# Attention scores: the low-part products of two heads on half the rows each, and both heads' score tiles filled together

## The chip, the cores and the metric

The kernel runs on 1 core of a Trainium2 chip. The metric is the device time of one execution, in microseconds. A core has a matrix engine (TensorE, PE in the profile; PEld is its weight load), VectorE (DVE), ScalarE (ACT), GpSimd (POOL), and a queue that issues DMAs (SyncE, SP). Each engine works through its own queue of instructions in order, and they wait for each other by semaphores.

## The reference, cut to what matters

The input `x` is 4 sequences of 1024 tokens of 256 numbers. Four residual blocks follow each other: a linear recurrence, a sparse feed-forward block (FFN), attention with 8 heads of 64, and the same FFN again. The change lies in the attention:

```python
q = (x @ Wq.T).reshape(b, t, N_HEADS, HEAD_DIM)
kv_latent = x @ Wkv_down.T                              # 64 numbers for each token
k = (kv_latent @ Wk_up.T).reshape(b, t, N_HEADS, HEAD_DIM)
v = (kv_latent @ Wv_up.T).reshape(b, t, N_HEADS, HEAD_DIM)
scores = jnp.einsum('bqhd,bkhd->bhqk', q, k) * HEAD_DIM ** (-0.5)
attn = jax.nn.softmax(scores, axis=-1)
out = jnp.einsum('bhqk,bkhd->bqhd', attn, v)
return out.reshape(b, t, N_HEADS * HEAD_DIM) @ Wo.T
```

## The kernel before

The kernel folds `Wk_up` into the query weights, so that all heads share one set of keys: the 64 latents of each token. For accuracy every factor of a product is split into a high part that TensorE multiplies exactly (`kh`) and the rest, a low part (`kl`). The latents are produced twice, one copy above the other, so `kh` and `kl` are tiles of 128 partitions by 1024 tokens whose halves hold the same 64 latents. The queries of one head `j` of a pair are a tile `qs[:, j, :]`, whose 64 rows of this head (rows 0 to 63 for `j = 0`, 64 to 127 for `j = 1`) hold the high part and whose other 64 rows hold the low part. A product `qs.T @ kh` over 128 rows is therefore (high + low of the queries) times the high part of the keys, and `qs.T @ kl` the same queries times the low part of the keys.

`Attention.heads` runs over the tokens of one sequence: 2 blocks of 512 tokens, 4 pairs of heads `g`, 4 query tiles `q` of 128 tokens; in all 128 such steps for the 4 sequences, each with two heads `j`, and so 256 score tiles. For one head the steps are:

- L881: four matmuls fill a score tile `sc` of 128 queries by 1024 keys in PSUM (two banks): two column halves `kb` with `kh`, then the two halves with `kl`. There are two buffers of `sc`.
- L885: VectorE takes the negated row maximum `nm`. For even `q`, L887 adds a constant to it.
- L889: ScalarE writes `pr`, the exponentials, and their sums. After this the `sc` buffer is free.
- Even `q` (`by_dma`): L892 and L893 split `pr` into two f16 parts `pd` on ScalarE and GpSimd, and L894 transposes them by DMA into `d`. Odd `q`: L900 transposes `pr` on TensorE into `ptp`, and L903 or L905 copies it into `p`.
- `values_sum` (L925) multiplies by the latents into `pmo` for both heads, the two heads in the two column halves of TensorE; L933 transposes the reciprocals of the sums into the same bank, L935 copies them, and L936 scales the result into `on`. It runs one step late.

Between these steps a generator schedule (`merge`) lets side work in: the FFN tiles `f1.tile` (top-32 search on VectorE, L674; products L170, L556), preparation of the next sequence, queries (`pmq`, L170; `qs`, L853), the output product (`pmy`, L170). The order in which the program is written is not yet the order of the queues: a scheduler that plays the program through a timeline decides the order of each engine's queue. `tc.high_priority()` raises the priority of what is issued in it, and `tc.issue_after(x)` puts an instruction behind `x` in the queue's order.

Of the kernel before, what the change touches and what calls it, by code (L numbers as in the profile page):

```python
# [21 lines left out]
P = 128  # L22
B = 4
T = 1024
# [6 lines left out]
HD = 64  # L31
# [148 lines left out]
class Banks:  # L180


    def __init__(self, pool, bufs):
        self.pool, self.bufs = pool, bufs
# [587 lines left out]

class Attention:
    def __init__(self, tc, x, ident, ident64, wqk, wvo, wd, sp, wp):
        self.nc, self.x, self.ident, self.ident64 = tc.nc, x, ident, ident64
        self.wqk, self.wvo, self.wd, self.sp, self.wp = wqk, wvo, wd, sp, wp
        self.hp = None
        self.k, self.xnt, self.qs, self.on = {}, {}, {}, {}

        self.sident = wp.tile([HD, HD], F32R, tag="sident", name="sident")  # L780
# [75 lines left out]
    def heads(self, b, psum):  # L856

        nc, sp, wp = self.nc, self.sp, self.hp  # L860
        kh, kl, la, lb = self.k[b]
        late, pending = [], []
        for nb, g, q in ((nb, g, q) for nb in range(2) for g in range(PAIRS) for q in range(4)):
            by_dma = q % 2 == 0
            if g == 0:
                self.on[b, nb, q] = wp.tile([P, PAIRS, P], F32, tag=f"on{q}", name=f"on{q}")
            qs = self.qs[b, nb, g]
            ssum = sp.tile([P, 2], F32, tag="ssum", name="ssum", bufs=4)
            if by_dma:
                pts = [wp.tile([P, 2 * TPB, P], F16, tag=f"d{j}", name=f"d{j}", bufs=2) for j in range(2)]  # L870
                parts = ((0, lb[0]), (TPB, lb[0]), (0, lb[1]))
                terms = [(v[:, c, :], i + c) for c in range(TPB) for i, v in parts]
            else:
                pts = [wp.tile([P, TPB, P], F32, tag=f"p{j}", name=f"p{j}") for j in range(2)]
                terms = [(la[:, c, :], c) for c in range(TPB)]
            for j in range(2):
                sc = psum.tile([P, T], "sc", "sc")
                for i, kk in enumerate((kh, kl)):
                    for kb in range(2):
                        sl = slice(kb * 512, (kb + 1) * 512)  # L880
                        nc.tensor.matmul(  # L881
                            sc[:, sl], qs[:, j, q * P : (q + 1) * P], kk[:, sl], start=(i == 0), stop=(i == 1)
                        )
                nm = sp.tile([P, 1], F32, tag="nm", name="nm", bufs=4)
                nc.vector.tensor_reduce(nm, sc, AX.X, ALU.max, negate=True)  # L885
                if by_dma:
                    nc.vector.tensor_scalar(nm, nm, PSHIFT * math.log(2.0), None, ALU.add)  # L887
                pr = wp.tile([P, T], F32, tag="pr", name="pr", bufs=3)
                nc.scalar.activation(pr, sc, AF.Exp, bias=nm, accum_out=ssum[:, j : j + 1])  # L889
                if by_dma:  # L890
                    pd = wp.tile([P, 2, T], F16, tag="pd", name="pd", bufs=2)
                    nc.scalar.copy(pd[:, 0, :], pr)  # L892
                    nc.gpsimd.tensor_tensor(pd[:, 1, :], pr, pd[:, 0, :], ALU.subtract)  # L893
                    nc.sync.dma_start_transpose(pts[j], pd.rearrange("p i k -> p (i k)"))  # L894
                else:
                    for half in range(2):
                        pt = psum.tile([P, 4, P], "t", "ptp")
                        for kk in range(4):
                            kc = 4 * half + kk
                            nc.tensor.transpose(pt[:, kk, :], pr[:, kc * P : (kc + 1) * P], self.ident)  # L900
                        dst = pts[j][:, 4 * half : 4 * half + 4, :]
                        if half == 0 and b == B - 1:
                            nc.vector.tensor_copy(dst, pt)  # L903
                        else:
                            nc.scalar.copy(dst, pt)  # L905
                if j == 0 and pending:
                    self.values_sum(*pending.pop(0), psum)
                if j == 1 and late and by_dma:
                    self.values_sum(*late.pop(0), psum)
                yield  # L910
            (late if by_dma else pending).append((pts, terms, ssum, self.on[b, nb, q][:, g, :]))
        for args in late + pending:
            self.values_sum(*args, psum)

    def values_sum(self, pts, terms, ssum, on, psum):

        nc, sp = self.nc, self.sp
        rs = sp.tile([P, 2], F32, tag="rs", name="rs")
        nc.vector.reciprocal(rs, ssum)
        rows = sp.tile([P, 2, HD], F32, tag="rows", name="rows")  # L920
        nc.gpsimd.tensor_copy(rows, rs[:, :, None].to_broadcast([P, 2, HD]))  # L921
        po = psum.tile([P, 2, P], "s", "pmo")
        for n, (v, c) in enumerate(terms):
            for j in range(2):
                nc.tensor.matmul(  # L925
                    po[j * HD : (j + 1) * HD, 0, :],
                    v,
                    pts[j][:, c, :],
                    start=(n == 0),
                    stop=(n == len(terms) - 1),  # L930
                )

        nc.tensor.transpose(po[:, 1, :], rows.rearrange("p j d -> p (j d)"), self.ident)  # L933
        rb = sp.tile([P, P], F32, tag="rb", name="rb", bufs=1)
        nc.scalar.copy(rb, po[:, 1, :])  # L935
        nc.vector.tensor_tensor(on, po[:, 0, :], rb, ALU.mult)  # L936
# [370 lines left out]
```

## Time and profile before

| | |
|---|---|
| median of 3 runs | 1532.92 us (1526.67 to 1534.85) |
| the profiled execution's own time | 1534.08 us |
| its span, first to last instruction | 1532.4 us |
| granted TensorE clock, mean | 0.937 of full speed |
| PE, DVE, ACT, POOL busy over the span | 85%, 77%, 66%, 44% |
| first to last score matmul (L881) | 377.9 us to 1294.7 us of the span |

The profile page lists busy time by engine, 40 time slices, DMA queues, the chain of waits that ended last, and the costliest groups of instructions: line, engine, operation, `out<-in` by the program's names, shapes, count, then busy time and mean nanoseconds of one, then the idle time of the engine just before them and what ended it. The time of a matmul is modelled and includes the time in which its results come out, while the next one already runs; the distance from start to start of two matmuls is what TensorE needs for one.

### The profile page before, as it was taken

To read this page: it belongs to the slowest core of one execution; us is meant where nothing else is said; L and a number is where in the kernel's file an instruction comes from. 1 tells how busy PE (TensorE), PEld (TensorE's weight loads), DVE (VectorE), ACT (ScalarE), POOL (GpSimd) and SP (SyncE) were. 2 spreads that over 40 slices of the span, in tenths; PEclk is the share of its full clock that TensorE was granted. 3 is DMA by queue.
4 is the path that set the end of the run, shared out by engine and by line. 5 is a ranking of instruction groups with operands and counts; after the bars stand their busy time and mean duration, and the time that the engine had idled before them with its cause. 6 is when DMAs were issued, how large, how long until landed. Compare 5 with 4: busy or idle time off the path is not lost. (4 is left out here: it accounts for less than half of the span.)

```text
span 1532.4 us, 28699 instructions
## 1 busy us (share of the span) xinstructions
PE 1295.5 (85%) x10136; PEld 960.3 (63%) x10136; DVE 1183.2 (77%) x3674; ACT 1017.3 (66%) x2148; POOL 681.6 (44%) x849
## 2 busy tenths in 40 slices
PE   5879998697898898888988989899999998666775
PEld 3635455376676766766766767677777776434454
DVE  8976665697878887878778687776676675499998
ACT  5353433466887877797778687877776776476664
POOL 2033332162545454544544543445443534067876
PEclk9989999699999999999999999999999999679888
DMA  3010000321454334434433335334445454000000
GB/s 117 26 47 15 19 23 21 123 94 56 76 98 89 64 76 74 73 74 80 84 73 69 68 72 87 62 71 84 70 75 92 73 95 83 1 15 24 22 25 28
DMA packets 288609, 96.51 MB, mean 63 GB/s; under 512 B 268233, under 2 KB 284626, under 8 KB 288466
## 3 DMA queue, kind: packets, MB, share of 16 engines
q1 hardware_dynamic: 283024, 88.50, 28.5%
q10 hardware_dynamic: 5442, 6.18, 1.2%
q8 instruction: 80, 1.31, 0.3%
q14 instruction: 63, 0.52, 0.1%
HBM read 16.01 MB, written 11.53 MB: 18 GB/s over the span
## 5 line engine op out<-in xcount | busy, mean ns | idle before, releaser
L893 POOL TENSOR_TENSOR pd<-pr,pd 128x1024 f16<-128x1024 f32 x128 | 273.3, 2141 | 247.5 <-ACT pd L892 183.2
L885 DVE TENSOR_REDUCE nm<-sc 128x1 f32<-128x1024 f32 x256 | 308.5, 1218 | 78.3 <-PE sc L881 76.9
L889 ACT ACTIVATE pr<-sc,nm 128x1024 f32<-128x1024 f32 x256 | 286.2, 1120 | 84.4 <-DVE nm L887 44.6
L881 PE MATMUL sc<-kh,qs 128*128 128x512 f32 x512 | 185.4, 440 | 26.3 <-ACT pr L889 18.7
L881 PE MATMUL sc<-kl,qs 128*128 128x512 f32 x512 | 163.2, 399 | 0.0
L905 ACT COPY p<-ptp 128x512 f32<-128x512 f32 x224 | 124.1, 591 | 47.6 <-PE ptp L900 39.5
L674 DVE MATCH_REPLACE8 wk<-m,wk 128x256 f32<-128x256 f32 x384 | 154.8, 406 | 0.1
L900 PE MATMUL ptp<-ident,pr 128*128 128x128 f32 x1024 | 140.1, 277 | 16.2 <-ACT pr L889 15.3
L674 DVE MAX8 m<-wk 128x8 f32<-128x256 f32 x384 | 150.2, 412 | 0.4
L925 PE MATMUL pmo<-p,la 128*64 128x128 f32 x2048 | 142.7, 287 | 5.5 <-ACT ft L524 2.9
L900 PEld LDWEIGHTS ptp<-ident,pr 128*128 128x128 f32 x1024 | 117.0, 141 | 39.2 <-ACT pr L889 25.9
L892 ACT CAST pd<-pr 128x1024 f16<-128x1024 f32 x128 | 133.4, 1056 | 5.8 <-DMA d<-pd 4.8
L925 PEld LDWEIGHTS pmo<-p,la 128*64 128x64 f32 x2048 | 121.8, 143 | 24.6 <-ACT ft L524 5.1
L881 PEld LDWEIGHTS sc<-kh,qs 128*128 128x128 f32 x512 | 85.8, 196 | 50.9 <-ACT pr L889 29.9
L881 PEld LDWEIGHTS sc<-kl,qs 128*128 128x128 f32 x512 | 97.7, 191 | 23.5 <-issue 1.4
L925 PE MATMUL pmo<-d,lb 128*64 128x128 f16 x3072 | 102.6, 222 | 8.0 <-DVE qs L853 2.6
L925 PEld LDWEIGHTS <-lb 128*64 128x64 f16 x3072 | 91.8, 111 | 25.8 <-issue 20.1
L628 POOL TENSOR_TENSOR ex<-ex,wk 128x512 f32<-128x512 f32 x61 | 77.7, 1273 | 58.5 <-DVE wk L674 50.6
L921 POOL COPY rows<-rs 128x128 f32<-128x128 f32 x128 | 36.1, 294 | 127.3 <-PE pmo L933 71.5
L936 DVE TENSOR_TENSOR on<-pmo,rb 128x128 f32<-128x128 f32 x128 | 36.5, 285 | 67.8 <-ACT rb L935 67.4
L699 PE MATMUL pf<-wf,vt 128*128 128x256 f32 x288 | 81.6, 424 | 4.1 <-ACT vt L697 3.4
L147 PE MATMUL pt<-ident,xn 128*128 128x128 f32 x256 | 47.7, 308 | 42.9 <-ACT xn L145 31.4
(306 smaller groups left out, 2779.6 us busy)
## 6 DMA issues: line engine op xcount, KB each, us to landing
tt<-ft SPq DMA_DIRECT2D x16, 256.0 KB
tt<-tt SPq DMA_DIRECT2D x8, 512.0 KB
out<-x SPq DMA_DIRECT2D x32, 128.0 KB
x<-in_x ACTq DMA_DIRECT2D x6, 512.0 KB
pf<-pfs SPq DMA_DIRECT2D x12, 256.0 KB
full<-pf SPq DMA_DIRECT2D x24, 128.0 KB
d<-pd SPq DMA_TRANSPOSE x128
wa<-in_w_attn SPq DMA_DIRECT2D x2, 640.0 KB
```

The costliest lines, as they stand in the source:

```text
L147: nc.tensor.transpose(pt[:, k, i * P : (i + 1) * P], xn[:, k * P : (k + 1) * P], ident)
L628: pool.tensor_tensor(ex, ex, wk, ALU.subtract)
L674: ins = make(*args).ins
L699: nc.tensor.matmul(dst, vt[:, k, :], w.wf[:, k, :], start=(k == 0 and bias is None), stop=(k == KD - 1))
L881: nc.tensor.matmul(sc[:, sl], qs[:, j, q * P : (q + 1) * P], kk[:, sl], start=(i == 0), stop=(i == 1))
L885: nc.vector.tensor_reduce(nm, sc, AX.X, ALU.max, negate=True)
L889: nc.scalar.activation(pr, sc, AF.Exp, bias=nm, accum_out=ssum[:, j : j + 1])
L892: nc.scalar.copy(pd[:, 0, :], pr)
L893: nc.gpsimd.tensor_tensor(pd[:, 1, :], pr, pd[:, 0, :], ALU.subtract)
L900: nc.tensor.transpose(pt[:, kk, :], pr[:, kc * P : (kc + 1) * P], self.ident)
L905: nc.scalar.copy(dst, pt)
L925: nc.tensor.matmul(po[j * HD : (j + 1) * HD, 0, :], v, pts[j][:, c, :], start=(n == 0), stop=(n == len(terms) - 1),)
```

## The change

The score products go into a new method `scores` that fills the tiles of both heads of a step before the first maximum is taken. The four products with `kh` come first, head 0 then head 1. The products with `kl` use only the 64 rows of the head's own high part: `qs[r, j, :]` and `kl[r, :]`, with `r` the rows 0 to 63 for head 0 and 64 to 127 for head 1. The term low part of the queries times low part of the keys is thereby left out. These four products alternate between the heads, and each is put directly behind the one before in the queue's order. In the diff, lines of `before.py` and `after.py` are the same apart from what is shown; the maximum, the exponential and all that follows keep their code (their line numbers change: L885 becomes L880, L887 L882, L889 L884, L925 L937).

```diff
 class Attention:
     def __init__(self, tc, x, ident, ident64, wqk, wvo, wd, sp, wp):
+        self.tc = tc
...
-            for j in range(2):
-                sc = psum.tile([P, T], "sc", "sc")
-                for i, kk in enumerate((kh, kl)):
-                    for kb in range(2):
-                        sl = slice(kb * 512, (kb + 1) * 512)
-                        nc.tensor.matmul(
-                            sc[:, sl], qs[:, j, q * P : (q + 1) * P], kk[:, sl], start=(i == 0), stop=(i == 1)
-                        )
+            scs = self.scores(qs[:, :, q * P : (q + 1) * P], kh, kl, psum)
+            for j, sc in enumerate(scs):
                 nm = sp.tile([P, 1], F32, tag="nm", name="nm", bufs=4)
                 nc.vector.tensor_reduce(nm, sc, AX.X, ALU.max, negate=True)
...
+    def scores(self, qs, kh, kl, psum):
+        nc, tc = self.nc, self.tc
+        scs = [psum.tile([P, T], "sc", "sc") for _ in range(2)]
+        halves = [slice(kb * 512, (kb + 1) * 512) for kb in range(2)]
+        for j in range(2):
+            for sl in halves:
+                last = nc.tensor.matmul(scs[j][:, sl], qs[:, j, :], kh[:, sl], start=True, stop=False).ins
+        with tc.high_priority():
+            for sl in halves:
+                for j in range(2):
+                    r = slice(j * HD, (j + 1) * HD)
+                    with tc.issue_after(last):
+                        last = nc.tensor.matmul(scs[j][:, sl], qs[r, j, :], kl[r, sl], start=False, stop=True).ins
+        return scs
```

## The prediction

> **What bounds the kernel now.** I read the busy shares first, then the stretch in which score products run (378 to 1300 us), then the costliest groups, then the chain of waits.
>
> ```profile
> PE 1295.5 (85%) x10136; PEld 960.3 (63%) x10136; DVE 1183.2 (77%) x3674; ACT 1017.3 (66%) x2148; POOL 681.6 (44%) x849
> ```
>
> ```profile
> 378.00:1300.00 922.00, 826.80 (x8284) 658.76 (x8285) 690.61 (x1717) 704.09 (x1370) 427.38 (x419) 0.98 0.42 77
> ```
>
> The second line is the attention stage (its length, then busy us and counts of PE, PEld, DVE, ACT and POOL, clock, DMA): 922 us, PE 90% busy, DVE 75%, ACT 76%, clock 0.98. It holds 128 steps of two heads, so 7.2 us a step. Nobody is full: 95 us of PE idle, and PE's busy time includes result latency. Which dependency matters is seen in the groups:
>
> ```profile
> L885 DVE TENSOR_REDUCE nm<-sc 128x1 f32<-128x1024 f32 x256 | 308.5, 1218 | 78.3 <-PE sc L881 76.9
> L889 ACT ACTIVATE pr<-sc,nm 128x1024 f32<-128x1024 f32 x256 | 286.2, 1120 | 84.4 <-DVE nm L887 44.6
> L881 PE MATMUL sc<-kh,qs 128*128 128x512 f32 x512 | 185.4, 440 | 26.3 <-ACT pr L889 18.7
> L881 PE MATMUL sc<-kl,qs 128*128 128x512 f32 x512 | 163.2, 399 | 0.0
> ```
>
> The longest idle of DVE ends with a score tile, that of ACT with the maximum, and PE's wait before scores ends with the exponential that frees the buffer. It is a ring: scores, maximum, exponential, buffer free. The chain shows both roles of the score products:
>
> ```profile
> 1279.13 1.89 PE pmo L925 x30
> 1281.02 0.26 PE pmo L933
> 1281.28 0.94 PE sc L881 x4
> 1282.25 1.24 DVE nm L885
> 1283.51 1.21 ACT pr L889 x2
> 1284.76 1.09 PE ptp L900 x8
> 1285.86 1.85 PE sc L881 x8
> 1287.71 0.44 PE ptp L900 x4
> ```
>
> At 1281.28 the tile is latency, since the maximum follows. At 1285.86 eight products are PE throughput, since PE itself goes on. Followed back over 420 to 1310 us, the chain lies on PE 396 us, DVE 252 us, ACT 152 us; score products hold 109 us, 470 of the some 980 matmuls (48%). Only 29 times does it pass from them to a maximum.
>
> **The change, part by part.** Before, a score matmul follows another every 0.231 us (1.85 / 8), so a step costs PE 8 x 0.231 = 1.85 us. After, the four `kh` products stay: 0.92 us. The four 64-row products cost what these rows bound:
>
> ```profile
> 381.07 1.08 PE L170 MATMUL pmq<-xnt,wqk 128*128 128x512 f32 x3
> ...
> 382.78 0.27 PE L835 MATMUL pv<-sident,kh 64*128 64x64 f32 x1
> 382.89 0.27 PE L835 MATMUL pv<-sident,kl 64*128 64x64 f32 x1
> 383.09 0.72 PE L881 MATMUL sc<-kh,qs 128*128 128x512 f32 x2
> ...
> 710.12 1.53 PE L925 MATMUL pmo<-d,lb 128*64 128x128 f16 x48
> ```
>
> Products on 64 rows already exist (`pv`, all on the same rows). They start 0.11 us apart though they move only 64 columns: that is one weight load of 128 columns after another. From the last one to the 128-row product at 383.09 it takes 0.20, so changing between 64 and 128 rows costs 0.09 us; the way in costs the same (0.318 against 0.231 in four of the starts). Two halves of the array at work at once are shown for columns: the 48 products of L925 take 1.53 us, pairs start 3 ns apart. For rows nothing is shown. Low end: pairs overlap fully, 2 x 0.231 + 2 x 0.09 = 0.64. High end: no overlap, 4 x 0.231 + 0.18 = 1.10. I take full overlap spaced by weight loads, as `pv` is the nearest row: starts at 0, 0.11, 0.23, 0.34, the last streams to 0.56, plus 0.18 = 0.74. PE work per step is 0.92 + 0.74 = 1.66, so 0.185 less: 128 x 0.185 = -24 us of PE work (ends -36 and +23).
>
> The Trainium skill, TensorE: Matmul & The Clock Gate, Part 3 (packing small matmuls), states that matmuls on different row groups run concurrently, about 4 ns apart; by it alone the four would take the low end, 0.64.
>
> Now the ring. The two `sc` buffers served single tiles: in the trace the second tile's products start 3.7 us after the first's on average, so DVE and ACT get a tile every half step. From the end of a tile's last product to the end of its exponential takes 3.95 us (mean of start and end times), with waiting in the queues of DVE and ACT; then 2.0 us on average pass before PE refills that buffer, so few refills are tight. After the change both tiles become ready together, and `kl` of either head needs the other's buffer. In the built program's queues the two maxima stand side by side in 98 of 128 steps (25 before), the two exponentials in 81 (22 before). In all 64 steps with even `q` the addition L887 for head 0 stands behind head 1's maximum (18 before), so that even the first exponential waits for both maxima. Such a step of before:
>
> ```profile
> 1262.18 2.36 DVE L885 TENSOR_REDUCE nm<-sc 128x1 f32<-128x1024 f32 x2
> ...
> 1264.45 0.14 DVE L887 TENSOR_SCALAR nm<-nm 128x1 f32<-128x1 f32 x1
> ...
> 1265.02 1.12 ACT L889 ACTIVATE pr<-sc,nm 128x1024 f32<-128x1024 f32 x1
> ...
> 1266.12 1.12 ACT L889 ACTIVATE pr<-sc,nm 128x1024 f32<-128x1024 f32 x1
> ```
>
> From the first maximum to the end of the second exponential: 1267.24 - 1262.18 = 5.06. All 11 such steps have a mean of 5.24, the 12 with odd `q` and adjacent maxima 4.20. That is what PE has to bridge, from the end of a pair of tiles until head 1's buffer is free. What stands on PE's new queue in between, at start-to-start times of the trace (transpose 0.11, L925 0.12 a product in f32 and 0.03 in f16, L170 0.115 or 0.225), is 4.55 us after an even step and 3.36 after an odd one, plus 0.46 for head 0's `kh` products. So 5.01 against 5.24 (short in 46 of 64) and 3.82 against 4.20 (short in 40 of 63).
>
> Added along the queue, with each score group starting when PE's work before it is done and its buffer is free: 807 us after, of which 718 are work and 89 stalls; before, with single tiles and 3.95 us, 784, of which 742 are work and 42 stalls. So stalls +47, PE work -24, sum +23 us. The rest of the stage (922 - 784 = 138 us, waits of other PE work) I take as unchanged; a longer stall there can hide some of them, which speaks for less than the sum. Ends of the stall term: with the shortest such steps (4.66, 3.56) stalls are about 44, +2; with half a microsecond more in DVE's queue (its mean delay now, product end to maximum, is 0.53) 143, +100.
>
> Queued behind the waiting score products on PE are transposes L900, L925 and side work, all of which the in-order queue holds up; on ACT the copies L905 and L935 stand behind the waiting exponentials. Side work on POOL and the transposing DMAs get the two `pd` of a step closer together (2.14 us each on POOL, 44% busy): nothing, while `values_sum` runs a step late; without that cover up to 2 us a step. Other stages are untouched. DVE and ACT instructions keep counts and sizes.
>
> A rule speaks against the change too: the skill's TensorEngine Tiling page, PSUM Bottleneck, says that tiling speeds TensorE but not the reading out of PSUM. By it alone the saved PE work would be worth 0 instead of 24 us wherever the maximum (1.22 us) and the exponential (1.12 us) are awaited.
>
> From the profiled execution's 1534.08 us (1.2 above the median of the runs) the forecast is 1534.1 + 23 = 1557, given as 1556 against the runs.
>
> **The rivals.** *PE throughput decides* (faster). For it: PE is 90% busy, and the chain passes from scores to PE itself far oftener than to DVE. The price: 48% of the saved work, 0.48 x 24 = 11 to 0.48 x 36 = 17, up to 0.48 x 59 = 28 if changes between row counts hide: 1506 to 1523, say 1517. Against it: the queue sums above. It decides if the second exponential ends under 4.4 us (3.96 mean work + 0.46) after the pair of tiles.
>
> *The two cancel*: 1527 to 1542, if stalls take the place of waits elsewhere.
>
> *The rows do not overlap*: four products at 0.231 plus changes, 1.10 instead of 0.74, 128 x 0.36 = 46 more: 1603. Against it: the column pairs.
>
> **How the numbers follow.** Forecast (stalls outweigh, 1542 to 1590): 0.50. PE decides: 0.25. Cancel: 0.15. No overlap: 0.10. Half a per cent, 7.7 us, is about what a measurement of this kernel can tell from no change (the three runs spread over 8 us). Faster 0.25, same 0.15, slower 0.60. The range reaches from inside the PE case, 1512 (the faster tenth is left out), to 1595, short of no overlap. The forecast's own range is 1542 to 1590.
>
> **What would show it.** Right: `kl` pairs start about 0.11 us apart and four take under 0.75 us; PE's idle before the score products, ended by the exponential, grows from 26 us to 70 or more; DVE's idle before the maximum stays or grows. Wrong: PE's idle there stays near 26 us and the stage gets shorter than 900 us (PE decides), or `kl` starts 0.23 us apart (no overlap).

## The result, and the profile after

The changed kernel takes 1608.4 us (1607.9 to 1612.0), the kernel before 1531.2 us in the same comparison: ratio 1.0506, 95% interval 1.0483 to 1.0530. It is 77 us slower. The profiled execution has a span of 1606.1 us.

The busy shares of the page of the changed kernel, and its score stretch by windows (length, then busy us and counts of PE, PEld, DVE, ACT and POOL, clock, DMA):

```profile
PE 1310.6 (82%) x10134; PEld 921.5 (57%) x10136; DVE 1177.8 (73%) x3674; ACT 1019.6 (63%) x2148; POOL 678.5 (42%) x849
```

```profile
376.00:1372.00 996.00, 842.88 (x8269) 619.25 (x8270) 684.97 (x1717) 704.02 (x1369) 423.15 (x418) 0.95 0.40 71
```

DVE, ACT and POOL do the same work as before. The score stretch is 74 us longer, which is nearly the whole difference. PE idles 153 us of it where it was 95, and it is busy 16 us longer (before: 827) although 4 of its 8 score products run in pairs.

The granted clock of the stretch fell from 0.98 to 0.95. The clock records of the trace stand at 0.50 for 107 us of the stretch, before for 41. In such pieces of the kernel before, two score products start 0.426 us apart in place of 0.231, and two transposes 0.213 in place of 0.109. PE is busy in 103 of the 107 us and in 39 of the 41, so half of the difference, some 32 of the 77 us, is the most that can be lost in this way. How much of it lies on the path, no run tests.

The costliest groups of the changed kernel (L880, L884, L918 and L924 answer to L885, L889 and the two L881 of before):

```profile
L880 DVE TENSOR_REDUCE nm<-sc 128x1 f32<-128x1024 f32 x256 | 303.2, 1217 | 77.5 <-PE sc L924 76.7
L884 ACT ACTIVATE pr<-sc,nm 128x1024 f32<-128x1024 f32 x256 | 285.0, 1117 | 106.1 <-DVE nm L880 58.2
L895 PE MATMUL ptp<-ident,pr 128*128 128x128 f32 x1024 | 150.2, 286 | 50.7 <-ACT pr L884 47.7
L918 PE MATMUL sc<-kh,qs 128*128 128x512 f32 x512 | 175.5, 446 | 18.3 <-ACT pr L884 17.4
L900 ACT COPY p<-ptp 128x512 f32<-128x512 f32 x224 | 125.4, 593 | 86.4 <-PE ptp L895 86.0
...
L924 PE MATMUL sc<-kl,qs 64*128 64x512 f32 x512 | 95.7, 452 | 0.0
```

The same page of the kernel before has for the transposes and their copies:

```profile
L905 ACT COPY p<-ptp 128x512 f32<-128x512 f32 x224 | 124.1, 591 | 47.6 <-PE ptp L900 39.5
...
L900 PE MATMUL ptp<-ident,pr 128*128 128x128 f32 x1024 | 140.1, 277 | 16.2 <-ACT pr L889 15.3
```

PE's idle before score products did not grow (26.3 to 18.3 us). It grew before the transposes, 16.2 to 50.7, and what they wait for is an exponential. Before the products with the latents (L925 before, L937 after) it grew from 13.5 to 33.4 us. The copies behind them on ACT wait 86 us in place of 48.

The products themselves do what they should. PE's timeline of the changed kernel, and of a kernel described below in which each head's two half-row products stand alone:

```profile
701.85 1.17 PE L918 MATMUL sc<-kh,qs 128*128 128x512 f32 x4
702.94 0.73 PE L924 MATMUL sc<-kl,qs 64*128 64x512 f32 x4
703.60 0.65 PE L895 MATMUL ptp<-ident,pr 128*128 128x128 f32 x4
```

```profile
702.49 0.73 PE L882 MATMUL sc<-kl,qs 64*128 64x512 f32 x2
703.15 0.39 PE L554 MATMUL pl<-linb,ones 128*128 128x512 bf16 x1
```

Four products in pairs take 0.66 us from the first to the next operation; two alone on the same rows take 0.66 as well. In the start times the two of a pair are 3 ns apart, the next pair follows after 0.334, and the operation after it 0.324 later.

An even step on VectorE and ScalarE in the changed kernel:

```profile
707.61 2.34 DVE L880 TENSOR_REDUCE nm<-sc 128x1 f32<-128x1024 f32 x2
...
709.88 0.27 DVE L882 TENSOR_SCALAR nm<-nm 128x1 f32<-128x1 f32 x2
710.11 1.11 ACT L884 ACTIVATE pr<-sc,nm 128x1024 f32<-128x1024 f32 x1 [1.82 <-DVE nm L882]
...
711.21 1.10 ACT L884 ACTIVATE pr<-sc,nm 128x1024 f32<-128x1024 f32 x1
```

ACT stands idle 1.82 us until both maxima and the first addition are done, then frees both buffers within 1.1 us of each other. What is queued behind the two exponentials gets its data in one burst.

**A measure for all runs.** From the start and end times I took, for each of the 256 tiles, how long its buffer is *held*: from the first product written into it to the end of the exponential that reads it; and how long it is then *free*, until the first product of the next tile. There are two buffers, so the stretch is 128 times (held + free). Before: 5.22 + 1.97 = 7.19, times 128 is 920 us. After: 6.47 + 1.31 = 7.78, times 128 is 996. A tile is held 1.25 us longer, and only 0.66 of that could be taken from the free time. The sum of the two gives the stretch by arithmetic and explains nothing by itself; the hold alone does not order the runs of the table below either (5.36 us goes with 1593 us, 6.60 with 1594). It says where a longer stretch sits.

### The profile page after: what moved, and what is told of

It is laid out like the page before. It is cut to its first block, busy times and chain, and to the rows that moved or that the text cites. A ratio compares the mean times of both kernels' runs of the same rounds, so it can differ in the third digit from the quotient of the medians.

```text
span 1606.1 us, 28818 instructions
## 1 busy us (share of the span) xinstructions
PE 1310.6 (82%) x10134; PEld 921.5 (57%) x10136; DVE 1177.8 (73%) x3674; ACT 1019.6 (63%) x2148; POOL 678.5 (42%) x849
## 3 DMA queue, kind: packets, MB, share of 16 engines
q8 instruction: 80, 1.31, 0.3%
## 4 chain that ended last, share of the span: by engine, by line
PE 42%; DVE 34%; ACT 13%; issue 6%; DMA 3%; POOL 2%; ACTq 0%; SPq 0%; DVEq 0%; POOLq 0%; another core or an unknown queue 0%
PE pmo L937 9%; DVE nm L880 8%; DVE wk L674 7%; DVE m L674 6%; PE sc L918 5%; PE ptp L895 5%; ACT pr L884 5%; PE sc L924 3%; PE po L437 2%; PE pmy L170 2%; PE pu L170 2%; DVE qs L854 1%; PE pz L452 1%; PE pt L147 1%; DMA d<-pd 1%
## 5 line engine op out<-in xcount | busy, mean ns | idle before, releaser
L880 DVE TENSOR_REDUCE nm<-sc 128x1 f32<-128x1024 f32 x256 | 303.2, 1217 | 77.5 <-PE sc L924 76.7
L884 ACT ACTIVATE pr<-sc,nm 128x1024 f32<-128x1024 f32 x256 | 285.0, 1117 | 106.1 <-DVE nm L880 58.2
L895 PE MATMUL ptp<-ident,pr 128*128 128x128 f32 x1024 | 150.2, 286 | 50.7 <-ACT pr L884 47.7
L918 PE MATMUL sc<-kh,qs 128*128 128x512 f32 x512 | 175.5, 446 | 18.3 <-ACT pr L884 17.4
L937 PE MATMUL pmo<-p,la 128*64 128x128 f32 x2048 | 159.2, 299 | 11.9 <-DVE qs L854 6.2
L937 PEld LDWEIGHTS pmo<-p,la 128*64 128x64 f32 x2048 | 133.1, 151 | 34.9 <-issue 9.0
L887 ACT CAST pd<-pr 128x1024 f16<-128x1024 f32 x128 | 131.6, 1053 | 0.3
L937 PE MATMUL pmo<-d,lb 128*64 128x128 f16 x3072 | 110.9, 229 | 21.5 <-DVE on L948 8.0
L937 PEld LDWEIGHTS <-lb 128*64 128x64 f16 x3072 | 98.3, 116 | 42.5 <-issue 35.6
L918 PEld LDWEIGHTS sc<-kh,qs 128*128 128x128 f32 x512 | 90.0, 204 | 43.4 <-ACT pr L884 30.0
L924 PE MATMUL sc<-kl,qs 64*128 64x512 f32 x512 | 95.7, 452 | 0.0
L556 PE MATMUL pl<-lint,xc_f 128*128 128x512 f32 x128 | 74.0, 666 | 10.4 <-ACT xc_f L587 10.4
```

Of the source, the lines that this page charges most:

```text
L918: last = nc.tensor.matmul(scs[j][:, sl], qs[:, j, :], kh[:, sl], start=True, stop=False).ins
L924: last = nc.tensor.matmul(scs[j][:, sl], qs[r, j, :], kl[r, sl], start=False, stop=True).ins
L937: nc.tensor.matmul(po[j * HD : (j + 1) * HD, 0, :], v, pts[j][:, c, :], start=(n == 0), stop=(n == len(terms) - 1),)
```

## The experiments

Two theories stood against each other. *Coupling*: a tile is complete only when the other head's buffer is free, so that both buffers are held longer and everything comes in bursts. *Half rows*: products on 64 rows, with their changes of row count, cost PE more than they save. A third came up on the way: *a new plan*, since every edit lets the planner order the queues anew.

| kernel | us | ratio to before, interval | held + free, us |
|---|---|---|---|
| before | 1531 | | 5.22 + 1.97 |
| changed | 1608.4 | 1.0506 (1.0483 to 1.0530) | 6.47 + 1.31 |
| joint, full rows (e1) | 1610.0 | 1.0508 (1.0488 to 1.0529) | 6.47 + 1.29 |
| single, half rows (e2) | 1593.1 | 1.0397 (1.0371 to 1.0422) | 5.36 + 2.31 |
| joint, addition first (e4) | 1593.9 | 1.0411 (1.0375 to 1.0447) | 6.60 + 1.08 |
| single, no low part (e6) | 1536.8 | 1.0035 (1.0019 to 1.0052) | 5.37 + 1.85 |
| order only (e7) | 1551.3 | 1.0101 (1.0066 to 1.0135) | 5.33 + 1.94 |
| before, due time (e9) | 1534.3 | 1.0013 (0.9996 to 1.0031) | 5.22 + 1.96 |
| changed, due time (e9) | 1618.3 | 1.0563 (1.0537 to 1.0590) | 6.47 + 1.38 |
| head by head (e10) | 1547.3 | 1.0093 (1.0074 to 1.0112) | 5.35 + 1.94 |
| one product moved (e14) | 1594.9 | 1.0413 (1.0396 to 1.0430) | 6.25 + 1.42 |
| same-head pairs (e12) | 1572.0 | 1.0248 (1.0223 to 1.0274) | 5.53 + 1.92 |
| priority (e13) | 1534.2 | 1.0008 (0.9987 to 1.0029) | 5.22 + 1.99 |

**Joint filling with full rows.** One part of the change alone, on the changed kernel:

```diff
-last = nc.tensor.matmul(scs[j][:, sl], qs[r, j, :], kl[r, sl], ...)
+last = nc.tensor.matmul(scs[j][:, sl], qs[:, j, :], kl[:, sl], ...)
```

> The changed kernel with the low-part products on all 128 rows again; both tiles still filled together and the four low-part products still side by side. Coupling theory (filling both heads' tiles together is what costs): no gain from going back to 128 rows. PE work a step 8 x 0.231 = 1.85 us in place of the measured 1.69 (0.231 x 3 + 0.326 + 0.665), 128 x 0.16 = 20 us more PE work of which about half is on the chain: 1608 + 10, 1605 to 1630. Rival, the 64-row products cost (changes of row count, drained array): back near the kernel before, 1520 to 1550.

1610.0 us. PE's order is nearly that of the changed kernel (24 of its 10134 matmuls stand elsewhere in the trace), and so is the time: filling both tiles together costs all 77 us, and the half rows give back less than can be told here, 1.6 us of the some 20 us of PE work that they save in this place.

**Half rows with single tiles.** The other part alone, on the kernel before:

```diff
+r = slice(j * HD, (j + 1) * HD) if i else slice(0, P)
-sc[:, sl], qs[:, j, q * P : (q + 1) * P], kk[:, sl], ...
+sc[:, sl], qs[r, j, q * P : (q + 1) * P], kk[r, sl], ...
```

> The kernel before, each head's tile filled by itself, with the low-part products on the 64 rows of the head's high part (low part of the queries times low part of the keys left out). No two heads are neighbours, so no overlap, and each of the 256 tiles changes row count twice at 0.095 us: 49 us more PE work. Coupling theory: about half of that on the chain, 1531 + 24 = 1555, 1538 to 1580, well under the changed kernel. Rival, the 64-row products cost: near or over the changed kernel, 1590 to 1630.

1593.1 us, more than coupling expected and at the rival's figure. PE's order is that of before but for 387 of 10136 matmuls, so the price comes with the half rows and hardly with a new plan. The expectation had only the changes of row count. The starts show a third cost: within a tile they are 0.326, 0.337 and 0.324 us apart where full rows have 0.232, 0.231 and 0.236. Alone on the same rows, one half-row product follows the other after 0.337 rather than 0.231. That is 0.29 us a tile, 74 us of PE work in all, beside 62 us of time. It is not shown that all 62 are this work: the clock stands at 0.50 for 95 us of the stretch (41 before), which can account for up to 26 of them. So half rows do cost, unless their neighbour lies on the other half.

**The order of the addition.**

```diff
+with self.tc.issue_after(shifted) if by_dma and j else nullcontext():
     nc.vector.tensor_reduce(nm, sc, AX.X, ALU.max, negate=True)
 if by_dma:
-    nc.vector.tensor_scalar(nm, nm, PSHIFT * math.log(2.0), None, ALU.add)
+    shifted = nc.vector.tensor_scalar(nm, nm, PSHIFT * math.log(2.0), None, ALU.add).ins
```

> The changed kernel with VectorE's queue put in another order on even steps: the second head's maximum is issued behind the first head's addition, so the first exponential need not wait for both maxima (in the changed kernel's queue the addition stands behind the second maximum in all 64 even steps). Theory that this order is the main cost: red start to end of the second exponential falls from 5.5 us on even steps to the 4.0 us of odd steps, 64 x 1.5 = 96 us of ring, most of it given back: 1530 to 1565. Coupling theory: order is a part only, the two tiles still become ready together: 1570 to 1600.

1593.9 us: 14 us back, near the upper end of what coupling expected. Head 0's tile is held 6.25 us on even steps in place of 7.20, but head 1's 7.61 in place of 7.22, and head 0's on odd steps 6.75 in place of 5.66. The addition behind both maxima is a part of the cost, and by this run a small one.

**Low-part products left out, single tiles.** The loop over `(kh, kl)` runs over `(kh,)` alone.

> The kernel before without the low-part products (the low part of the keys is left out): 512 matmuls of 0.231 us less, 118 us of PE work. It shows what PE work in this place is worth when nothing else is changed. If PE throughput is on the chain as read from it (48%): 1531 - 57 = 1474, 1455 to 1490. If the ring is what counts, each tile is ready 0.46 us earlier too, and about the same comes out; if neither PE nor the tile's latency counts, over 1510.

1536.8 us, no gain where 118 us of PE work are gone: the outcome named last, though the half rows with single tiles show that added PE work does count. PE's busy time in the stretch fell by 70 us, the stretch did not shorten:

```profile
377.00:1303.00 926.00, 756.74 (x7759) 588.89 (x7760) 690.07 (x1717) 699.64 (x1370) 425.03 (x419) 0.92 0.42 76
```

The plan is another one for 3883 of PE's other 9624 matmuls, and with shorter score work it brings the two tiles of a step closer: 2.85 us from maximum to maximum, 3.5 before; exponentials side by side in 40 steps, 22 before. The clock is 0.92, at 0.50 for 143 us in place of 41, which can hide up to 41 us of a gain. Whether this and the order ate all of it, I did not test.

**Order alone, and a due time.** First the instructions of the kernel before, written in the changed kernel's order without priority and without the fixed order, then one due time of side work moved in either kernel:

```diff
-start = 1 + 6.75 * n if n < TPB else ...
+start = 1 + 6.5 * n if n < TPB else ...
```

> Exactly the instructions of the kernel before (low-part products on 128 rows), but written in the changed kernel's order (both heads' products before the first maximum) and with no priority and no fixed order, so that the planner separates the two tiles again (adjacent maxima in 24 of 128 steps, 25 before). Only the queues' order differs, by some 1800 of 11790 PE entries. Theory that a new plan by itself costs (the plan of the kernel before is a lucky or tuned one): 1560 to 1600. Coupling theory: single tiles again, so as before: 1525 to 1545.

> The kernel before with one due time of side work moved (FFN tiles of the first sequence every 6.5 steps in place of 6.75): same instructions, another plan for part of the queues (some 1400 of 11790 PE entries, the first sequence above all). New-plan theory: 1540 to 1580. Coupling theory: 1525 to 1540.

> The changed kernel with one due time of side work moved (FFN tiles of the first sequence every 6.5 steps in place of 6.75), as was done to the kernel before, where it made 2 us. If the joint filling costs through its structure, the time stays at 1600 to 1616; if the changed kernel only met an unlucky plan, it moves by more than 15 us, downwards most likely.

1551.3, 1534.3 and 1618.3 us: +1.0% and +0.1% on the kernel before, +0.6% on the changed one. The first lies between the ranges of its two theories. These three new plans move the time by 3 to 20 us, not by 77, which speaks against the changed kernel being merely an unlucky plan. The expectation of 1600 to 1616 for the last was passed by 2 us.

**A third score buffer**, in both kernels; the transposes' banks pay for it:

```diff
-pt = psum.tile([P, 4, P], "t", "ptp")
+pt = psum.tile([P, 4, P], "s", "ptp")
-{"sc": 2, "t": 2, "s": 2}
+{"sc": 3, "s": 2}
```

> The kernel before with three score buffers in place of two; the banks come from the transposes' own two buffers, which now share the two of the side work. Control for the next run. Coupling theory: single tiles were hardly short of buffers, the shared banks cost: 1530 to 1590.

> The changed kernel with three score buffers, banks as in the run before: head 0's next tile can be filled while both tiles of this step are in use, and head 1's next tile waits for head 0's exponential, not for head 1's. If the ring of the two buffers is what the joint filling costs, the distance to its control with three buffers falls well under the 77 us seen with two, to 0 to 30 us. If the cost lies in both tiles becoming ready together (maxima and exponentials side by side, transposes late), the distance stays at 50 to 90 us.

1630.5 us (ratio 1.0639, 1.0606 to 1.0672) and 1665.3 (1.0851, 1.0830 to 1.0872). The shared banks cost 98 us by themselves, so the control is poor; the distance between the two falls from 77 to 35 us, just over the bound that was set. So the joint filling still costs with a third buffer, about half as much. Inconclusive by itself.

**Head by head, and one product moved.** Both tiles stay ahead of the first maximum, with priority and a fixed order, all on 128 rows as in e1; the order is head 0 high, head 0 low, head 1 high, head 1 low. The second kernel moves one product of this (both written as lists):

```diff
-order = [(0,0,0), (0,0,1), (0,1,0), (0,1,1), (1,0,0), (1,0,1), (1,1,0), (1,1,1)]   # j, low part, column half
+order = [(0,0,0), (0,0,1), (0,1,0), (1,0,0), (1,0,1), (0,1,1), (1,1,0), (1,1,1)]
```

> Both tiles are still written before the first maximum, with priority and a fixed order, but head by head: head 0 high and low products, then head 1, all on 128 rows. PE does the work of the joint kernel with full rows; only head 0 no longer waits for head 1's high products and buffer. In the built queues maxima stand side by side in 45 of 128 steps (96 in the joint kernel with full rows), eight products without a gap in 69 (83). Theory that the cost is in both tiles becoming ready together: most of the 77 us comes back, 1535 to 1565. Rival, that neighbouring score products on PE (a long block that holds up side work and transposes) are the cost: 1580 to 1610.

> The head by head kernel (1547 us) with one of its eight products moved: head 0's last low-part product stands behind head 1's two high products, so that head 0's tile again is complete only when head 1's buffer has been free. All products on 128 rows, PE's work the same. Theory that the time a score buffer is held decides (5.2 us a tile before, 5.35 head by head, 6.45 in both joint kernels): the hold goes back to 6.2 or more and the time to 1595 to 1615. Rival, that it is the side by side low-part products or the long block on PE: 1540 to 1560.

1547.3 and 1594.9 us. Putting head 0's low-part products ahead of head 1's high ones takes 63 of the 77 us back from e1, at the same PE work. Moving one of the eight back so that head 0 must again wait for head 1's buffer costs 48 us (expected 1595 to 1615). Transposes and score products of the two pages, head by head first:

```profile
L921 PE MATMUL sc<-kh,qs 128*128 128x512 f32 x512 | 184.6, 441 | 23.5 <-ACT pr L884 12.6
...
L895 PE MATMUL ptp<-ident,pr 128*128 128x128 f32 x1024 | 142.1, 279 | 16.3 <-ACT pr L884 13.5
```

```profile
L921 PE MATMUL sc<-kh,qs 128*128 128x512 f32 x512 | 189.3, 451 | 36.0 <-ACT pr L884 26.5
...
L895 PE MATMUL ptp<-ident,pr 128*128 128x128 f32 x1024 | 142.0, 280 | 33.1 <-ACT pr L884 29.8
```

PE's idle before these two is 40 us in one and 69 in the other, ended by exponentials for the most part. The hold is 5.35 and 6.25 us. The low-part products stand in no pairs in either, so neither pairs nor row counts play a part. The moved product also lets the planner put the maxima side by side again, in 82 of 128 steps (45 head by head): waiting and bunching come together, and I could not part them. Nor is the moved product the only difference: some 4300 of PE's 10134 matmuls stand in another order, and the clock is at 0.50 for 58 us in place of 34, worth 12 us at most. What stands against a chance plan is the grouping of all runs of the table: with 128 rows throughout, the kernels in which a head's tile is complete without the other's buffer, in all but a few of their steps, take 1531 to 1551 us, and all in which it is not, on half rows or full ones, 1594 to 1618.

**Pairs within one head.** On the kernel before, GpSimd copies the high part of the queries to the other 64 rows, and one head's two low-part products use one half each, at high priority and in a fixed order:

```diff
+nc.gpsimd.tensor_copy(qd[other, :], qs[mine, j, :])
...
+h = j if kb == 0 else 1 - j
+r = slice(h * HD, (h + 1) * HD)
+src = qs[r, j, :] if kb == 0 else self.qd[b, nb, g][r, :]
+... src[:, q * P : (q + 1) * P], kl[r, sl], start=False, stop=True
```

> Another way to half rows: single tiles as before, but GpSimd copies the high part of the queries to the other 64 rows as well (two copies of 64 by 512 for each pair of heads and block), so that one head's two low-part products lie on different row halves and overlap without the other head. By the measured starts a tile costs 0.316 + 0.326 + 0.003 + 0.324 in place of 0.316 + 0.232 + 0.231 + 0.236: 46 ns less, 256 x 0.046 = 12 us of PE work, so 1515 to 1535 by the staggering theory if the copies hide and the new plan costs nothing; a new plan alone has cost 2 to 19 us, so 1520 to 1550. If half rows themselves were the cost: over 1580.

1572.0 us, slower than expected. The two do start 3 ns apart, but the operation behind them starts 0.43 us later, not 0.324 as in the changed kernel, so that a tile costs 1.07 us (0.315 + 0.326 + 0.003 + 0.427) and saves nothing over 1.015. Why the way out is 0.1 us longer here is open. The 0.056 us a tile make 14 us, of 38 by the ratio. In 29 of the 256 tiles the two do not stand next to each other in PE's order; what the rest is, was not tested.

**Freeing the buffers sooner.** On the kernel before, maximum, addition and exponential at high priority.

> The kernel before with maximum, addition and exponential at high priority, which is the other direction: nothing is added or left out, the planner is only asked to free the score buffers sooner. Theory that the hold decides also below 5.2 us: the hold falls to about 5.0 and the time by 5 to 25 us, 1507 to 1527. Theory that at 5.2 us a buffer is free 2 us on average and no longer short: no gain, 1525 to 1550 with the usual scatter of a new plan.

1534.2 us, no difference that can be told: the hold stayed at 5.22. No version here beats the kernel before.

## Why the prediction was wrong

**The direction was right, and so was the coupling of the two buffers. The size was not, and neither was the place of the wait.** 1556 us was forecast, in a range of 1512 to 1595; 1608 was measured. The forecast's sum was +47 us of stalls and -24 us of PE work.

*PE work.* The four half-row products were put at 0.74 us with the changes; the starts give 0.095 + 0.665 = 0.76. The pairs overlap, but not in the way assumed: the two of a pair start 3 ns apart and not 0.11, the second pair 0.334 after the first and not 0.23. That the totals agree is partly luck. As an amount of work the term came out; its worth did not. e1 shows that in the joint kernel the saving is worth 1.6 us. The sum took all 24. What PE work is worth in the kernel before stays open: 74 us more go with 62 us of time (e2), 118 us less gain nothing (e6).

*The stall term* is the step that failed: +47 forecast, +77 found (e1, which has no PE saving in it). Two things were mis-sized. The first is the chain from the end of the tiles to the end of the second exponential, put at 4.72 us on average. From the first maximum on this was right, 4.75 (5.51 on even steps, 4.00 on odd). But VectorE begins 0.37 us late on average (0.13 in e1), which makes 5.12. The prediction had this term and its price, half a microsecond more in DVE's queue for +100, and it had measured a mean delay of 0.53; the sum itself put it at nothing. In proportion, 0.37 us would make the stall term about +87 and the 0.13 of e1 about +61: an estimate from the prediction's own two values.

Second, the chain began at the last product. A buffer is taken from its first. Head 0's tile, begun early, now waits half filled for head 1's buffer: from the start of its first product to that of its last 2.26 us pass (2.29 in e1) where it was 0.92. From there to the end of its exponential it takes no longer than before (4.17 us, 4.30 before). For head 1 it is the other way round: 0.99 us to the last product (0.84 before), then 5.52 (4.36 before). So the hold grew from 5.23 to 6.43 us for head 0 as well as from 5.20 to 6.51 for head 1. The prediction charged the wait for head 1's buffer to PE alone, and named no term for the buffer that it keeps. It had no term for the clock either. How the 30 us that were missing divide among these three is not shown.

One reading of the prediction does not come out of the trace: its 12 odd steps with adjacent maxima average 4.75 us (median 4.28), not 4.20. It did no harm, as the changed kernel took 4.00.

*"The rest of the stage unchanged"* was wrong too. PE is in order, and transposes stand ahead of the next score products in its queue; they wait for the same late exponentials. Their idle grew by 35 us, while the idle before the score products, which the walk along the queue charged, shrank by 8. For this reason the signs named in the prediction misled: PE's idle before the score products was to grow to 70 us or more if it was right, and to stay near 26, with a stage under 900 us, if PE decides. It fell to 18, and the stage took 996. The wait had moved to the instruction in front.

**The rivals.** *PE throughput decides* fell: the stretch got longer, not shorter than 900 us. Its price, 48% of the PE work saved, was met neither in the changed kernel (1.6 us of some 20, e1) nor in the kernel before (nothing of 118, e6). *Cancel* fell. *The rows do not overlap* fell by the 3 ns, although its time, 1603, is the nearest. The page TensorE: Matmul & The Clock Gate of the Trainium skill, Part 3, is borne out for pairs of row groups; its 4 ns agree with 3 ns here. By its span alone four products would have taken 0.64 with the changes; 0.76 was measured, since the second pair follows after 0.334 and not 0.231. TensorEngine Tiling, PSUM Bottleneck, pointed to the right place: nothing in reading the tiles out became faster (the maximum takes 1.217 us, 1.218 before, the exponential 1.117, 1.120 before).

## What to carry to other kernels

Before two accumulations are interleaved so that they can share the matrix engine, count how long each PSUM buffer is held, from the first product written to the end of its last reader, and multiply by the tiles over the buffers: if little of the stage is left free, what is saved on the engine is not worth an added wait. Look for the new wait on every instruction that stands ahead of the blocked one in an in-order queue, not only on the blocked one. And an edit that makes a planner order the queues anew moved the time by 0.1 to 1.0% in the three runs here that did little else, so one part of a change should also be run with the queues nearly unchanged, as e1 and e2 do.

## What the hardware showed beyond what was expected

Two half-row products on the same rows follow each other after 0.337 us, against 0.231 for full rows, and each change between 64 and 128 rows adds about 0.09 to 0.1 us: half rows without a neighbour on the other half cost 0.29 us a tile here. Pairs start 3 ns apart, but pair after pair needs 0.334 us. The granted clock of the score stretch fell from 0.98 to 0.95 in the changed kernel and was 0.98 again head by head. It does not simply follow PE's idle: with single tiles on half rows PE idles 64 us of the stretch, less than the 95 of before, and the clock is 0.95 as well. Head by head, then single tiles on half rows:

```profile
376.00:1310.00 934.00, 833.51 (x8285) 656.86 (x8287) 683.91 (x1718) 702.75 (x1372) 427.26 (x419) 0.98 0.43 76
376.00:1359.00 983.00, 919.04 (x8270) 640.24 (x8271) 692.54 (x1717) 705.89 (x1370) 426.90 (x419) 0.95 0.40 72
```
